# A graph attention layer on one core: the last product's output written by ScalarE, x added by accumulating transfers, the first norm tile by tile, and a fixed table as the order

## The chip, the cores and the metric

The kernel runs on one core of a Trainium2 chip. Its engines are TensorE (PE in the profile; its weight loads have a row of their own, PEld), VectorE (DVE), ScalarE (ACT), GpSimd (POOL) and SyncE (SP). Each works off its own list of instructions in order, and they meet only at semaphores. Transfers are issued from two lists: SP's (the hardware queue) and GpSimd's (the software queue, the one whose transfers can add to what stands at the destination). The metric is the time of one execution on the device in microseconds, the median of several.

## The reference

One pre-normalised layer of graph attention over 32 graphs of 512 nodes with 512 features, in float32:

```
h = jnp.maximum(_layernorm(x, axis=-1), 0.0)
x = x + _L0_gnn_ref(adj, h, W1, att_src1, att_dst1, b1, W2, att_src2, att_dst2, b2)

def gat_layer(x, mask, W, a_src, a_dst, bias, concat):
    xl = (x @ W).reshape(B, N, H, F)
    asrc = jnp.einsum('bnhf,hf->bnh', xl, a_src)
    adst = jnp.einsum('bnhf,hf->bnh', xl, a_dst)
    e = jax.nn.leaky_relu(asrc[:, :, None, :] + adst[:, None, :, :], NEG_SLOPE)
    e = jnp.where(mask[..., None], e, NEG_INF)
    attn = jax.nn.softmax(e, axis=1)
    out = jnp.einsum('bsdh,bshf->bdhf', attn, xl)
    return out (heads side by side, or their mean) + bias

mask = (adj > 0) | jnp.eye(N, dtype=bool)[None]
h = jax.nn.elu(gat_layer(x, mask, W1, att_src1, att_dst1, b1, concat=True))
h = gat_layer(h, mask, W2, att_src2, att_dst2, b2, concat=False)
```

The first layer has 4 heads of 256 features, the second one head of 512. What matters for the change is the last line of each graph: the second layer's product of attention and features, divided by the softmax's sums, plus x.

## The kernel before, in words

The work of a graph is cut into 128-row tiles (four of nodes, four of features). For each graph b the program does, in this order of dependence: `load` x and normalise it (`norm`: statistics on VectorE, 1/sqrt(var + eps) as a power on GpSimd, then scale, shift and relu on ScalarE; `norm_turn` turns the tiles for TensorE); `masks` (the adjacency as 0 or a large negative number, written to DRAM once); the first projection `project1`; the first layer's softmaxes (class `Soft`, one per head) and their products `gather1`; the second projection `project2`; the second layer's softmax `second_layer` and its product `gather2`, which ends with x added and the rows stored. A softmax tile p gets its mask by an accumulating transfer of 512 KB on GpSimd's list (`p<-dm`), and the sums by which it divides go through DRAM to be spread over the partitions (`drr<-rr`, then `rr<-drr`, on SP's list; `as<-das` likewise for the scores).

Most large products are done in seven block products instead of eight (`sevens`, a Strassen-Winograd scheme): products 1 to 7 are chains of matmuls into PSUM banks; some sums are kept in the bank, and a bank's sum goes on into another bank by a copy on ScalarE. Those copies are the rows `ACT ACTIVATE mm<-mm` of the profile. A bank is 2 KB per partition, and there are eight: a chain can start only when its bank has been read out.

`gather2` does so for the last product. Its inner function `put` (L1487) takes finished blocks of 128x256 from the bank to the output tile: on VectorE, bank times `share` (one over the softmax's sum) plus what stands in the tile. What stands there is x, which `residual` (L1435) has loaded ahead by SP into one of the four t tiles (or, for the last graphs, into tiles of adj, x and mt). After the row's last put SP stores it. The last graph goes through `gather2_plain` (L1514), which has no seven products.

The loop after L1560 interleaves the second half of one graph with the first of others. It doesn't run the work but adds jobs (engine, cost, what it reads and writes) to a `Program` (L223). `order` (L299) then sets the lists: a list scheduler with a clock of its own, in which each job has a modelled duration, each hand-over a modelled delay, and the two queues share a modelled wire. Where several jobs of an engine are ready, the smaller number in `PLACES` (L63) goes first; the places of one middle graph are repeated for all of them, each a turn later. So the lists of two middle graphs need not be alike. `emit` (L373) writes the instructions in that order, and the waits follow from what is read and written. All engines' instructions have one line each in the profile: L531 TensorE, L514 ScalarE, L517 VectorE, L520 SP's transfers, L525 GpSimd's transfers, L770 the power.

Of the kernel before, what the change touches and what calls it, by code (L numbers as in the profile page):

```python
# [10 lines left out]
F32 = mybir.dt.float32  # L11
# [4 lines left out]
OP = mybir.AluOpType  # L16
# [28 lines left out]
class Banks(Slots):  # L45
# [171 lines left out]
)  # L217
LATE = {
   
}  # L220

# [1488 lines left out]
```

## Time and profile before

| what | us |
|---|---|
| runs shown | 2767.8, 2768.55, 2772.54 |
| median | 2768.55 |
| profiled execution | 2769.33 |
| its span | 2767.6 |
| granted clock, mean | 0.999 |
| ScalarE puts of the last product | none |
| accumulating transfers on GpSimd's list | 314 masks of 512 KB |
| t<-in_x_dram on SP's list | 124 of 256 KB |

The profiled execution's own time is 1.73 us more than its span; what follows is counted from the span's start. In a group's row stand line, engine, operation, output<-input with the buffers' names, the shape, the count, and behind the bar the busy time, the mean in ns, and the idle time ahead with who ended it. In a timeline row stand the start, the duration, the engine and operation, and in brackets the idle time before and who ended it. A matmul's record is longer than the distance to the next one, since they are pipelined.

### The profile page before, as it was taken

To read this page: it belongs to the slowest core of one execution; us is meant where nothing else is said; L and a number is where in the kernel's file an instruction comes from. 1 tells how busy PE (TensorE), PEld (TensorE's weight loads), DVE (VectorE), ACT (ScalarE), POOL (GpSimd) and SP (SyncE) were. 2 spreads that over 40 slices of the span, in tenths; PEclk is the share of its full clock that TensorE was granted. 3 is DMA by queue.
4 is the path that set the end of the run, shared out by engine and by line. 5 is a ranking of instruction groups with operands and counts; after the bars stand their busy time and mean duration, and the time that the engine had idled before them with its cause. 6 is when DMAs were issued, how large, how long until landed. Compare 5 with 4: busy or idle time off the path is not lost. (4 is left out here: it accounts for less than half of the span.)

```text
span 2767.6 us, 42320 instructions
## 1 busy us (share of the span) xinstructions
PE 2742.4 (99%) x12924; PEld 2371.8 (86%) x12924; DVE 2558.2 (92%) x6732; ACT 2229.1 (81%) x4907; POOL 313.1 (11%) x356
## 2 busy tenths in 40 slices
PE   7999999999999999999999999999999999999999
PEld 6788888888888888888888888888888888888887
DVE  8999999999999999999999999999999999999996
ACT  5978888778887788877888877888778788788883
POOL 0110111101111111111011111111111111101110
PEclk9999999999999999999999999999999999999999
DMA  8657766667666667667676766766676767767563
GB/s 232 176 157 182 203 167 184 187 176 194 182 183 179 182 176 196 178 175 195 173 201 172 182 187 178 192 186 180 180 188 175 201 167 180 195 165 208 162 171 112
DMA packets 375864, 502.14 MB, mean 181 GB/s; under 512 B 222804, under 2 KB 227668, under 8 KB 375636
## 3 DMA queue, kind: packets, MB, share of 16 engines
q1 hardware_dynamic: 329844, 332.68, 42.4%
q0 software_dynamic: 45792, 166.74, 25.1%
q8 instruction: 103, 1.69, 0.3%
q14 instruction: 125, 1.02, 0.1%
HBM read 316.41 MB, written 51.31 MB: 133 GB/s over the span
## 5 line engine op out<-in xcount | busy, mean ns | idle before, releaser
L531 PE MATMUL mm<-w_sb,hs 128*128 128x257 f32 (+3 forms) x2908 | 667.0, 367 | 5.1 <-ACT mm L514 3.3
L531 PEld LDWEIGHTS mm<-w_sb,hs 128*128 128x128 f32 x2908 | 539.7, 190 | 87.7 <-ACT mm L514 6.7
L525 POOL DMA_DIRECT2D p<-dm x314 | 273.2, 875 | 2295.0 <-DVE p L517 764.3
L531 PE MATMUL mm<-w_sb,ht 128*128 128x258 f32 x2112 | 528.6, 382 | 2.7 <-ACT mm L514 2.5
L531 PE MATMUL mm<-p,xl 128*128 128x258 f32 (+1 forms) x1984 | 495.8, 383 | 0.1
L531 PE MATMUL mm<-w_sb,h 128*128 128x257 f32 x2056 | 477.8, 379 | 0.0
L517 DVE SCALAR_TENSOR_TENSOR p<-rr,z 128x512 f32<-128x512 f32 (+1 forms) x636 | 456.0, 742 | 2.4 <-DMA rr<-drr 2.4
L531 PEld LDWEIGHTS mm<-w_sb,ht 128*128 128x128 f32 x2112 | 393.7, 190 | 63.6 <-ACT mm L514 6.4
L514 ACT ACTIVATE p<-p,z 128x512 f32<-128x512 f32 (+1 forms) x636 | 433.4, 720 | 17.7 <-DVE p L517 12.4
L531 PEld LDWEIGHTS mm<-w_sb,h 128*128 128x128 f32 x2056 | 389.0, 189 | 58.4 <-ACT xl L514 0.5
L531 PEld LDWEIGHTS mm<-p,xl 128*128 128x128 f32 x1984 | 367.2, 190 | 52.7 <-issue 6.0
L514 ACT ACTIVATE mm<-mm 128x257 f32<-128x257 f32 (+2 forms) x498 | 169.8, 347 | 269.2 <-PE mm L531 236.2
L514 ACT ACTIVATE l<-as,z 128x512 f32<-128x512 f32 x516 | 354.4, 716 | 30.8 <-DMA as<-das 30.7
L514 ACT ACTIVATE l<-l,low 128x512 f32<-128x512 f32 x516 | 370.3, 721 | 7.6 <-DVE low L517 6.7
L517 DVE CUSTOM_DVE_ANT_1 l<-l,mt 128x512 f32<-128x512 f32 x516 | 346.2, 681 | 28.4 <-ACT l L514 27.4
L514 ACT ACTIVATE xl<-mm 128x258 f32<-128x258 f32 (+2 forms) x748 | 269.3, 382 | 91.4 <-PE mm L531 89.8
L514 ACT ACTIVATE h<-mm,b_sb 128x256 f32<-128x256 f32 (+1 forms) x504 | 231.0, 480 | 77.3 <-PE mm L531 76.6
L531 PE MATMUL mm<-t,hs 128*128 128x258 f32 (+1 forms) x992 | 246.1, 380 | 0.0
L517 DVE TENSOR_TENSOR xl<-xl,mm 128x258 f32<-128x258 f32 x372 | 155.3, 419 | 57.9 <-PE mm L531 48.3
L531 PEld LDWEIGHTS mm<-t,hs 128*128 128x128 f32 x992 | 185.8, 190 | 25.5 <-DVE t L517 0.2
L531 PE MATMUL mm<-xl,p 128*128 128x258 f32 (+2 forms) x752 | 189.7, 388 | 1.0 <-ACT h L514 0.6
L517 DVE SCALAR_TENSOR_TENSOR h<-xr,h 128x512 f32<-128x512 f32 x256 | 172.2, 683 | 6.1 <-ACT xr L514 6.1
(137 smaller groups left out, 3706.2 us busy)
## 6 DMA issues: line engine op xcount, KB each, us to landing
p<-dm POOLq DMA_DIRECT2D x314, 512.0 KB, 5.0
rr<-drr SPq DMA_DIRECT2D x159, 512.0 KB
x<-in_x_dram SPq DMA_DIRECT2D x129, 256.0 KB
adj<-in_adj_dram SPq DMA_DIRECT2D x128, 256.0 KB
as<-das SPq DMA_DIRECT2D x64, 512.0 KB
t<-in_x_dram SPq DMA_DIRECT2D x124, 256.0 KB
out_dram<-t SPq DMA_DIRECT2D x124, 256.0 KB
dm<-m SPq DMA_DIRECT2D x64, 256.0 KB
```

What stands on the lines that cost most here:

```text
L514: prog.add("ACT", cost, reads, writes, lambda: nc.scalar.activation(*a, **k))
L517: prog.add("DVE", cost, reads, writes, lambda: f(*a, **k))
L525: lambda: nc.gpsimd.dma_start(to, at, accum_op=OP.add), size,
L531: f(*a, **k)
```

## The change

**What `put` does.** Of the six products of `gather2` that reach the output tile, 3 and 7 stay on VectorE (bank times share, added to the tile), the others become a scaled copy on ScalarE that overwrites the tile. That moves 248 operations (31 graphs, 8 in each) from VectorE to ScalarE and leaves 124 on VectorE.

**Where x comes from.** `residual` loads x only for the last graph. For the others, after a row's last put, a transfer on GpSimd's list adds x from DRAM to the finished tile, and SP's store waits for it: 124 transfers of 256 KB leave SP's list, and 124 accumulating ones of the same size enter GpSimd's.

**The first norm.** For graph 0 the epsilon, the power and the shift run for each of the four tiles by itself (128x1 instead of 128x4), so each of these three instructions becomes four.

**Room.** The identity matrix for the turns takes the place of a work tile (`hx`) that is first used later; the constant `diag` is made from it there.

**The order.** The scheduler with its clock, the delays and the wire is gone, and so is the table `LATE`. `PLACES` has new numbers in a finer unit, and each engine's list is its jobs sorted by their place. All middle graphs then have the same list. The matmuls are the same in number and width.

```diff
-            dma(XLOAD, [x2_key(b, 0, 0)], halves, xr, x[b, d * P : (d + 1) * P, :])
+            if b == B - 1:
+                dma(XLOAD, [x2_key(b, 0, 0)], halves, xr, x[b, d * P : (d + 1) * P, :])
+            else:
+                for c in range(2):
+                    prog.alias(xk + (c,), [xk, xk + (c,)])
             XR[b].append((places[d], xk, xr))
...
             if n in (2, 5):
                 dve(TINY, [bk], [sk], nc.vector.reciprocal, share, ps[:, M : M + 1])
-            dve(
-                PUT, [bk, sk, xk + (c,)], [xk + (c,)], nc.vector.scalar_tensor_tensor,
-                to, ps[:, :M], share, to, op0=OP.mult, op1=OP.add,
-            )
+            if n in (3, 7):
+                dve(
+                    PUT, [bk, sk, xk + (c,)], [xk + (c,)], nc.vector.scalar_tensor_tensor,
+                    to, ps[:, :M], share, to, op0=OP.mult, op1=OP.add,
+                )
+            else:
+                act(COPY, [bk, sk, xk], [xk + (c,)], to, ps[:, :M], AF.Copy, scale=share)
 
             upper[u[0]] -= n in (2, 3)
             if n == 4 or r == 0 and upper[u[0]] == 0:
                 upper[u[0]] = -1
+                halves = [xk, xk + (0,), xk + (1,)]
+                accumulate(XADD, halves, halves, xt, x[b, d * P : (d + 1) * P, :])
                 dma(STORE, [xk, xk + (0,), xk + (1,)], (), out[b, d * P : (d + 1) * P, :], xt)
...
-        every = [sk + (t,) for t in range(NT)]
-        rstd = st[:, :, S + A]
-        dve(TINY, every, every, nc.vector.tensor_scalar_add, rstd, st[:, :, S + 1], EPS)
...
+        for ts in ([t] for t in range(NT)) if b == 0 else [range(NT)]:
+            every = [sk + (t,) for t in ts]
+            at = slice(ts[0], ts[-1] + 1)
+            rstd = st[:, at, S + A]
+            dve(TINY, every, every, nc.vector.tensor_scalar_add, rstd, st[:, at, S + 1], EPS)
+            prog.add(
+                "POOL", 1.0, every, every,
+                lambda r=rstd, n=len(every): nc.gpsimd.tensor_tensor(r, r, half[:, :n], op=OP.pow),
+            )
...
-    identf = sbuf.tile([P, P], F32, name="identf")
+    identf = hx[SMALL[0]][:, 0, :]
...
-                [xk], [pk], 0.44,
+                [xk, ("hx", SMALL[0])], [pk], 0.44,
...
     def order(self):
-        jobs, rank = self.jobs, self.ranks()
...
-                release(j, lambda s: t + jobs[j][1] + self.latency(j, s))
+        jobs, rank, done = self.jobs, list(self.ranks()), []
+        after, left = [[] for _ in jobs], [len(job[2]) for job in jobs]
...
+        lines = {e: [] for e in self.ENGINES}
+        for j in sorted(range(len(jobs)), key=lambda j: (rank[j], j)):
+            lines[jobs[j][0]].append(j)
+        lines = [deque(q) for q in lines.values()]
+        while any(lines):
+            q = min((q for q in lines if q and not left[q[0]]), key=lambda q: rank[q[0]])
+            j = q.popleft()
             done.append(j)
+            for k in after[j]:
+                left[k] -= 1
         return done
...
 PLACES = (
-    -21124, -21123, -21187, -21124, -19956, -19941, -19942, -21301, -19903, -19904, -18841, -19897, -6146, 6511,
...
 )
```

What moves in the lists is shown at three places. The first is VectorE's start before: four tiles of statistics, then one epsilon (`TENSOR_SCALAR`) and one shift for all, around the first score sums (`xr,w_sb<-w_sb,p`).

```order
L517 BN_STATS stats_123<-x_90 128x6
L517 BN_AGGR stats_123<-stats_123 128x2
L517 BN_STATS stats_123<-x_88 128x6
L517 BN_AGGR stats_123<-stats_123 128x2
L517 BN_STATS stats_123<-x_91 128x6
L517 BN_AGGR stats_123<-stats_123 128x2
L517 BN_STATS stats_123<-x_89 128x6
L517 BN_AGGR stats_123<-stats_123 128x2
L517 TENSOR_SCALAR stats_123<-stats_123 128x4
L517 SCALAR_TENSOR_TENSOR xr_96,w_sb<-w_sb,p_102 128x256
```

The same start with the change:

```order
L473 BN_STATS stats_122<-x_90 128x6
L473 BN_AGGR stats_122<-stats_122 128x2
L473 TENSOR_SCALAR stats_122<-stats_122 128x1
L473 BN_STATS stats_122<-x_88 128x6
L473 BN_AGGR stats_122<-stats_122 128x2
L473 TENSOR_SCALAR stats_122<-stats_122 128x1
L473 BN_STATS stats_122<-x_87 128x6
L473 BN_AGGR stats_122<-stats_122 128x2
L473 TENSOR_SCALAR stats_122<-stats_122 128x1
L473 BN_STATS stats_122<-x_89 128x6
L424 TENSOR_SCALAR diag<-hx_79 128x128
L473 SCALAR_TENSOR_TENSOR stats_122<-stats_122 128x1
```

The epsilon of each tile now follows its own statistics, and the first tile's shift (the last row) stands ahead of the fourth tile's aggregation. The second place is GpSimd's list in a middle graph, where before there were only masks and one power for each graph (`L770`).

```order
L525 DMA p_102<-dm_120 128x1024 x2
L525 DMA p_103<-dm_122 128x1024 x2
L525 DMA p_104<-dm_122 128x1024 x2
L770 TENSOR_TENSOR stats_123<-stats_123,half 128x4
L525 DMA p_102<-dm_122 128x1024 x2
L525 DMA p_103<-dm_122 128x1024 x2
```

And with the change (t_105 to t_108 are the output tiles):

```order
L481 DMA p_103<-dm_120 128x1024 x2
L481 DMA t_105<-in_x_dram 128x512
L481 DMA t_107<-in_x_dram 128x512
L481 DMA p_101<-dm_120 128x1024
L481 DMA t_108<-in_x_dram 128x512
L481 DMA t_106<-in_x_dram 128x512
L729 TENSOR_TENSOR stats_123<-stats_123,half 128x4
L481 DMA p_101<-dm_120 128x1024
L481 DMA p_102<-dm_120 128x1024 x2
```

The four accumulating transfers of a graph stand together, and one mask's two halves (p_101) are parted by two of them. The third place is SP's list around the stores of a middle graph, before:

```order
L520 DMA rr_114<-drr_118 128x1024
L520 DMA out_dram<-t_108 128x512
L520 DMA x_90<-in_x_dram 128x512
L520 DMA out_dram<-t_106 128x512
L520 DMA out_dram<-t_109 128x512
L520 DMA out_dram<-t_107 128x512
L811 DMA_TRANSPOSE x_91<-adj_94 128x8x128
L520 DMA drr_119<-rr_115 4x8x32
L811 DMA_TRANSPOSE x_90<-adj_95 128x8x128
L520 DMA rr_115<-drr_119 128x1024
```

And with the change:

```order
L476 DMA rr_114<-drr_118 128x1024
L476 DMA x_87<-in_x_dram 128x512
L476 DMA out_dram<-t_108 128x512
L476 DMA drr_117<-rr_113 4x8x32
L476 DMA out_dram<-t_105 128x512
L476 DMA out_dram<-t_107 128x512
L476 DMA out_dram<-t_106 128x512
L770 DMA_TRANSPOSE x_87<-adj_94 128x8x128
L770 DMA_TRANSPOSE x_88<-adj_93 128x8x128
L476 DMA rr_113<-drr_117 128x1024
```

The broadcast of a softmax's sums (`rr_113<-drr_117`) now stands behind three stores and two transposes, and each store behind its tile's accumulating transfer; before, the write and the read of the broadcast both stood behind the stores, and the stores waited only for VectorE.

More of the change, by code (lines that the diff above doesn't have):

```diff
@@ L2 @@
 from contextlib import ExitStack
-from heapq import heappop, heappush
 import concourse.bass as bass
@@ L63 @@
 PLACES = (
[153 rows of a table removed]
-)
-LATE = {
-}
[197 rows of a table added]
+)
 class Program:
-    CROSS, SAME = 0.15, 0.07
-    PAIRS = {("PE", "ACT"): 0.21, ("PE", "DVE"): 0.21, ("DVE", "POOL"): 0.58, ("POOL", "DVE"): 0.4}
-    AHEAD, MASK, OTHER = 3.5, (0.75, 1.84), 0.76
-    KIND = {
-        0.3: (0.39, 1.21, 0.1, 0.9),
-        0.76: (0.81, 1.62, 0.33, 0.64),
-        0.77: (0.44, 1.45, 0.2, 0.82),
-        0.9: (0, 1.72, 1.0, 0.41),
-        0.92: (0.48, 2.18, 0.24, 0.89),
-        0.94: (-0.2, 1.76, 0.21, 0.6),
-        1.09: (1.58, 1.56, 0.53, 0.59),
-        1.84: (0.48, 2.18, 0.24, 0.89),
-        2.23: (0.58, 1.62, 0.53, 0.4),
-    }
     ENGINES = "PE", "ACT", "DVE", "POOL", "SP"
@@ L267, in alias @@
         self.readers[key] += [self.writer[k] for k in others if k in self.writer]
-    def latency(self, a, b):
-        if self.jobs[a][0] != self.jobs[b][0]:
-            return self.PAIRS.get((self.jobs[a][0], self.jobs[b][0]), self.CROSS)
-        return 0.0 if self.jobs[a][0] == "PE" else self.SAME
-    def kind(self, j):
-        if self.jobs[j][0] == "POOL":
-            return self.MASK
-        return self.KIND.get(self.jobs[j][4], self.KIND[self.OTHER])
     def ranks(self):
@@ L286, in ranks @@
         turn = sum(job[1] for job in self.jobs[first : first + each] if job[0] == "PE")
-        rank, self.place = [], []
         for j in range(n):
             if j < first:
-                v, i = j, 0
+                yield PLACES[j] / 10000
             elif j < last:
-                v, i = first + (j - first) % each, (j - first) // each + 1
+                yield PLACES[first + (j - first) % each] / 10000 + turn * ((j - first) // each + 1)
             else:
-                v, i = first + each + j - last, (last - first) // each + 1
-            self.place.append(v)
-            rank.append(PLACES[v] / 100 + turn * i)
-        return rank
+                yield PLACES[first + each + j - last] / 10000 + turn * ((last - first) // each + 1)
     def order(self):
-        jobs, rank = self.jobs, self.ranks()
-        n = len(jobs)
-        after = [[] for _ in range(n)]
+        jobs, rank, done = self.jobs, list(self.ranks()), []
+        after, left = [[] for _ in jobs], [len(job[2]) for job in jobs]
         for j, job in enumerate(jobs):
@@ L305, in order @@
                 after[d].append(j)
-        left = [len(job[2]) for job in jobs]
-        ready_at, self.start, done = [0.0] * n, [0.0] * n, []
-        free, soon, ready = dict.fromkeys(self.ENGINES, 0.0), defaultdict(list), defaultdict(list)
-        wires, now, behind = {"SP": deque(), "POOL": deque()}, 0.0, {"SP": 0.0, "POOL": 0.0}
-        for j in range(n):
-            if not left[j]:
-                heappush(soon[jobs[j][0]], (0.0, j))
-        def release(j, at):
-            for s in after[j]:
-                ready_at[s] = max(ready_at[s], at(s))
-                left[s] -= 1
-                if not left[s]:
-                    heappush(soon[jobs[s][0]], (ready_at[s], s))
@@ L321, in step @@
-        def step(until):
-            nonlocal now
-            busy = [q for q in wires if wires[q] and wires[q][0][1] <= now]
-            speed = dict.fromkeys(wires, 1.0)
-            if len(busy) == 2:
-                speed["SP"], speed["POOL"] = self.kind(wires["SP"][0][0])[2:]
-            event, which = until, None
-            for q in wires:
-                if wires[q]:
-                    j, since, todo = wires[q][0]
-                    t = now + todo / speed[q] if q in busy else since
-                    if t < event:
-                        event, which = t, q
-            for q in busy:
-                wires[q][0][2] -= (event - now) * speed[q]
-                behind[q] -= (event - now) * speed[q]
-            now = event
-            if which in busy:
-                j = wires[which].popleft()[0]
-                release(j, lambda s: event + self.kind(j)[1] + LATE.get(self.place[j], 0) / 100)
-            return which is not None
@@ L344, in order @@
-        while len(done) < n:
-            t, e = float("inf"), None
-            for q in self.ENGINES:
-                if ready[q]:
-                    at = free[q]
-                elif soon[q]:
-                    at = max(free[q], soon[q][0][0])
-                else:
-                    continue
-                if q in wires:
-                    at = max(at, now + behind[q] - self.AHEAD)
-                if max(at, now) < t:
-                    t, e = max(at, now), q
-            if step(t):
-                continue
-            while soon[e] and soon[e][0][0] <= t:
-                k = heappop(soon[e])[1]
-                heappush(ready[e], (rank[k], k))
-            j = heappop(ready[e])[1]
-            self.start[j] = t
-            free[e] = t + jobs[j][1]
-            done.append(j)
-            if jobs[j][4] is not None:
-                wires[e].append([j, free[e] + self.kind(j)[0], jobs[j][4]])
-                behind[e] += jobs[j][4]
-            else:
-                release(j, lambda s: t + jobs[j][1] + self.latency(j, s))
+        lines = {e: [] for e in self.ENGINES}
@@ L443, in tile_gat @@
     nc.scalar.preload_act_table_set("natural_log_exp_and_others")
-    identf = sbuf.tile([P, P], F32, name="identf")
-    make_identity(nc, identf)
-    diag = sbuf.tile([P, P], BF16, name="diag")
-    nc.vector.tensor_scalar(diag, identf, -1.0, BIG, op0=OP.add, op1=OP.mult)
     half = sbuf.tile([P, NT], F32, name="half")
@@ L468, in tile_gat @@
     hx = {n: sbuf.tile([P, 3, P], F32, name=f"hx{n}") for n in SMALL}
+    identf = hx[SMALL[0]][:, 0, :]
+    make_identity(nc, identf)
+    diag = sbuf.tile([P, P], BF16, name="diag")
+    nc.vector.tensor_scalar(diag, identf, -1.0, BIG, op0=OP.add, op1=OP.mult)
     rs = sbuf.tile([P, 2, 2, 2], F32, name="rs")
@@ L764, in norm @@
             dve(TINY, [sk + (t,)], [sk + (t,)], nc.vector.bn_aggr, st[:, t, S : S + A], st[:, t, :S])
[L765 to L776 removed]
+        for ts in ([t] for t in range(NT)) if b == 0 else [range(NT)]:
[7 more added lines that the diff above has]
+            )
+            shift = st[:, at, S]
+            dve(
+                TINY, every, every, nc.vector.scalar_tensor_tensor,
+                shift, shift, -1.0, rstd, op0=OP.mult, op1=OP.mult,
+            )
         ST[b] = sk, st
```

12 lines of the change are left out of this document (3 added, 9 removed), and 349 rows, old and new, of the table PLACES.

## The prediction

> **What bounds the kernel now.** I read the page's busy table first, then the same table cut into five stretches, then who waits for whom in the long middle stretch, and last the timelines where TensorE stands.
>
> ```profile
> span 2767.6 us, 42320 instructions
> PE 2742.4 (99%) x12924; PEld 2371.8 (86%) x12924; DVE 2558.2 (92%) x6732; ACT 2229.1 (81%) x4907; POOL 313.1 (11%) x356
> 0.00:50.00 50.00, 36.09 (x171) 31.07 (x172) 39.96 (x164) 23.57 (x48) 2.86 (x8) 1.00 0.94 271
> 50.00:250.00 200.00, 198.47 (x879) 161.38 (x878) 184.58 (x515) 169.33 (x370) 26.41 (x28) 0.99 0.65 170
> 250.00:2620.00 2370.00, 2365.14 (x11250) 2062.82 (x11248) 2216.07 (x5766) 1950.71 (x4294) 271.66 (x306) 1.00 0.69 183
> 2620.00:2700.00 80.00, 78.79 (x367) 67.32 (x367) 74.17 (x180) 64.09 (x150) 10.39 (x12) 1.00 0.63 170
> 2700.00:2768.00 68.00, 63.88 (x264) 49.26 (x262) 43.40 (x110) 21.38 (x49) 1.75 (x2) 0.99 0.33 106
> ```
>
> After the bounds of a stretch come its length, the busy time of TensorE (matmuls, weight loads), VectorE, ScalarE and GpSimd, the clock, and the share of the DMA engines. TensorE is busy 99% of the span at full clock, so no work taken from VectorE shortens anything by itself; only TensorE's idle time can be won or lost. It is 25.2 us: 13.9 in the first 50, 1.53 up to 250, 4.86 in the whole middle, 1.21 up to 2700 and 4.1 behind it. The change leaves every matmul in place (12,960 passes in both instruction lists; the trace lacks a few records), so these are the whole field for a gain. A loss has no such limit.
>
> The waits of the middle stretch (engine and line, whom it waited for; us in total, times, longest):
>
> ```profile
> PEld mm L531 <- ACT mm L514: 10.7, 17, 1.6
> PE mm L531 <- ACT mm L514: 4.4, 8, 1.2
> DVE t L517 <- PE mm L531: 5.9, 20, 0.3
> ACT mm L514 <- DVE t L517: 26.4, 28, 1.8
> POOL p L525 <- DVE p L517: 591.0, 92, 15.5
> ACT p L514 <- DMA p<-dm: 5.2, 8, 1.4
> ```
>
> What TensorE waits for there is ScalarE's copies of one matmul bank into another, and nothing else of weight. Here is how one such wait comes about, and how another is fed by a late mask:
>
> ```profile
> 852.53 1.95 ACT L514 ACTIVATE l<-as,z 128x512 f32<-128x512 f32 x3 [2.27 <-DMA as<-das]
> 854.38 0.52 ACT L514 ACTIVATE mm<-mm 128x129 f32<-128x129 f32 x2
> 854.69 2.01 PE L531 MATMUL mm<-w_sb,ht 128*128 128x258 f32 x8 [0.81 <-ACT mm L514]
> 2351.29 8.79 DMA p<-dm
> 2360.10 1.16 ACT p L514 x2
> 2361.34 0.27 ACT mm L514
> 2361.65 0.49 PE L531 MATMUL mm<-w_sb,hs 128*128 128x129 f32 x2 [0.45 <-ACT mm L514]
> 2385.74 233.85 PE mm L531 x1104
> ```
>
> At 852.53 three long operations stand ahead of the copy, because their input landed late, and TensorE stands 0.81 us. At 2360 the same with two exponentials behind a late mask. So the order on ScalarE's list sets the small stalls. A wait also costs more than the idle shows: a matmul record lasts some 0.38 us and the next starts after 233.85/1104 = 0.212, so up to 0.17 us of each of these 25 waits is hidden under the matmul before it. The middle thus holds 4.86 + 25 x 0.17 = about 9 us at most.
>
> **The start.**
>
> ```profile
> 8.15 0.66 DVE L517 BATCH_NORM_STATS2 stats<-x 128x6 f32<-128x512 f32 x1
> 9.31 1.04 POOL L770 TENSOR_TENSOR stats<-stats,half 128x4 f32<-128x4 f32 x1 [8.00 <-DVE stats L517]
> 11.20 2.23 ACT L514 ACTIVATE x<-x,stats 128x512 f32<-128x512 f32 x3 [9.16 <-DVE stats L517]
> 13.21 0.43 DVE L517 SCALAR_TENSOR_TENSOR xr<-w_sb,p 128x256 f32<-128x256 f32 x1 [1.30 <-DMA p<-in_L_gnn_att_dst_dram]
> 12.06 2.82 PE L531 MATMUL mm<-identf,x 128*128 128x128 f32 x12 [12.06 <-ACT x L514]
> 14.67 5.92 PE L531 MATMUL mm<-w_sb,ht 128*128 128x258 f32 x24
> 20.43 0.60 PE L531 MATMUL mm<-identf,x 128*128 128x128 f32 x4
> ```
>
> Before, one power on GpSimd (9.31) waits for all four tiles' statistics, the first normalisation starts at 11.20 and TensorE at 12.06. Tile by tile, three of the four powers can run before the last tile's statistics end at about 9.0. Even if each 128x1 power takes the 1.04 us of the 128x4 one, the four end by about 10.4 and the first normalisation starts soon after the second tile. But the transposes were not the last gate: the score sum that waits for att_dst starts at 13.21 and takes 0.43, and the first product needs it. That landing is a load in the same place of SP's list. So the products can start near 13.7 in place of 14.67, 1.0 us; and with four transposes done by then the group at 20.43 no longer stands in the dense run, 0.44 to 0.60. I take 1.5 us. Bounds: 0, if VectorE's later sums set the pace as the waits of this stretch allow, and 14.67 - 12.06 = 2.6, if nothing but the transposes did.
>
> **The puts moved to ScalarE, and x's way into the tile.**
>
> ```profile
> L517 DVE SCALAR_TENSOR_TENSOR t<-mm,rs,t 128x256 f32<-128x256 f32 x360 | 165.6, 474 | 8.9 <-PE mm L531 7.6
> L514 ACT ACTIVATE mm<-mm 128x256 f32<-128x256 f32 x124 | 46.5, 375 | 70.3 <-PE mm L531 68.5
> L514 ACT ACTIVATE h<-mm,b_sb 128x256 f32<-128x256 f32 x496 | 225.7, 477 | 77.0 <-PE mm L531 76.6
> L525 POOL DMA_DIRECT2D p<-dm x314: 862/862/1217, 63.0 to 2718.9; - x157
> p<-dm POOLq DMA_DIRECT2D x314, 512.0 KB, 5.0
> q1 hardware_dynamic: 329844, 332.68, 42.4%
> q0 software_dynamic: 45792, 166.74, 25.1%
> ```
>
> VectorE loses 248 operations of 0.474, 117.6 us, and goes from 92% to 88% busy. ScalarE gains 248. A scaled copy to SBUF is not in this trace; its bounds are the bank copy of the same size (375 ns) and the activation with a bias that reads a bank and writes SBUF (477). That is 93 to 118 us, and 81% becomes 84 to 85%. The second is the nearer row, as it writes to SBUF too. On TensorE's path neither counts: a bank is released 0 to 0.1 us later or earlier, and the 26.4 us that ScalarE stood behind VectorE's puts (28 times, once a graph) goes, because the put ahead of that copy is now its own.
>
> GpSimd gains 124 accumulating transfers of 256 KB. Issuing one costs 862 ns (the middle value of the masks' 314), 107 us, so 11% becomes 15%. On the wire a mask takes 25.1% x 2767.6 / 314 = 2.2 us of all 16 engines (what little else shares that queue is counted with it); x's transfer moves half the bytes of a mask's row, so 1.1 to 2.2. SP loses 124 loads: its queue moved 332.68 MB in 42.4% of 2767.6 us, so 0.26 MB takes 0.9 us. The net is +0.2 to +1.3 us times 124, 1 to 6 points of a 69% share. An accumulate lands in about 4 to 5 us by the mask's 5.0, and the store that follows it waits that long on SP's list. Nothing of TensorE's reads the tile; what could be hurt is what stands behind it: the next masks on GpSimd, and the broadcasts on SP. In the new order the four accumulates stand in one group, with one mask pair parted by them, where there was none; by the order's lists 100 passes or more of TensorE lie between a row's last product and the reuse of its tile, 100 x 0.212 = 21 us, against 5 + 2 for accumulate and store. The masks of the second layer have some 73 passes, 15 us, between their last use and their next. Value for the middle from this: 0, between -1 and +2, the latter if five covers run out by one 0.4 us wait each.
>
> The page "SBUF — State Buffer" of the Trainium skill, section "SBUF: two separate sides", speaks against this move: a transfer issued from GpSimd starves for descriptors while VectorE holds the shared port, and SP's or ScalarE's queue is advised. By its case of 3.1 us in place of 0.62 an issue would be an estimated 2.5 us later, four accumulates 10 us, and the masks behind them would have 5 of 15 us left. The trace disagrees so far: with VectorE at 92% the issues stay at 862 ns and the longest at 1217. I sum by the trace.
>
> **The order.** The list scheduler with modelled times goes, and each engine's list is a fixed table. In the lists, places where a ScalarE piece must finish while only one product chain (four passes, 0.85 us) runs are 173, down from 380, VectorE's 157 against 155. That is the kind of place of the 25 waits above. If waits fall with places, 9 x (1 - 173/380) = 4.9 us go; some new ones come, since the new list can't give way to whatever lands first in a model. I take -4, with 0 to -9 as bounds. For the run-in (50 to 250, idle 1.53, and the rest of the first 50, about 1.9 behind the start) I take -1.2, between +1.5 and -3.4; for 2620 to 2700 -0.5 of its 1.21.
>
> **The end.** The final product and store stay:
>
> ```profile
> 2749.97 13.91 PE L531 MATMUL mm<-xl,p 128*128 128x512 f32 x32
> 2763.92 0.69 DVE L517 TENSOR_TENSOR t<-mm,t 128x512 f32<-128x512 f32 x1 [1.89 <-PE mm L531]
> 2756.64 8.33 SPq L520 DMA_DIRECT2D out_dram<-t  x4
> ```
>
> The last graph still loads x and adds it on VectorE, so its tail is the same 3.7 us. Its x tiles must wait for the stores of the graph before, which now wait for their accumulates: +0.2, up to +0.5.
>
> **Sum.** -1.5 (start) - 1.2 - 4 - 0.5 + 0.2 = -7.0 on the profiled execution's 2769.33: 2762.3. The median of the runs shown, 2768.55, is 0.78 lower, so 2761.6.
>
> **Rivals.**
>
> *Only the start is won.* The table merely trades one set of small stalls for another: -1.5, 2767.0. For it: 4.86 of 2370 us is little, and each fixed place that comes late is late in every graph. Against it: the places with one chain of cover halve.
>
> *Masks and broadcasts behind x (slower).* GpSimd's queue is in order; an accumulate that waits for its row's last put holds the masks behind it, and a store that waits for an accumulate holds the softmax's broadcast on SP. A late mask cost 0.45 us at 2361 with 8.79 us of wire in the chain above. One to two such places in each of 29 middle graphs are +13 to +26, +20 in the middle, less the start's 1.5: about 2787. For it: masks went out 92 times in wait of VectorE, up to 15.5 us each, so the queue is used late. Against it: 21 us of cover, and ScalarE waited for a mask only 8 times, 5.2 us in all. It decides once a mask's cover falls below its 5 us landing.
>
> *GpSimd's issues stretch (slower).* With five issues in a row, each at the longest 1217 in place of 862 ns, a mask goes out 1.8 us later. If that uses up one cover in each graph, 31 x 0.45 = +14, less the start's 1.5: about 2781. Against it: the 314 issues of this trace reach 1217 at the longest, beside a VectorE that will be less busy. This is where the skill's page would lead, if its rule held here.
>
> *ScalarE's copies come later (slower).* At 85% a copy that frees a bank stands behind one more put of 0.48 us. Cover is 0.85 us in 173 places; if one place in each graph loses 0.3 us, +9: about 2776. Against it: the puts are placed apart from the copies, and 26.4 us of ScalarE's standing behind VectorE end.
>
> *The change does not do what it says*, in that x's transfers take the wire from SP's loads. At +6 points of 69% no stretch but the first (94%, without such transfers) is near full; 2769 at most, and I count it with the first rival.
>
> **How the numbers follow.** A difference under 0.2% (5.5 us: 2763.0 to 2774.1) can't be told from no change. Forecast 0.60, with its own range 2755 to 2767; about three quarters of it lies below 2763.0, so 0.45 faster, 0.15 same. Only the start 0.19, same but for 0.01 faster. Masks and broadcasts 0.11, stretched issues 0.03, both slower. ScalarE's copies 0.07: slower 0.06, same 0.01. Together faster 0.46, same 0.34, slower 0.20. The range 2754 to 2778 holds the forecast's own range, the second case and that of the copies, and leaves out most of the masks' and the stretched issues' cases, 0.12, and about 0.04 of the forecast's gains.
>
> **What would show it.** Right: first normalisation before 10 us and products by 13.8; ScalarE at 84 to 85%, VectorE at 88%; TensorE's idle in 250 to 2620 below 3 us with fewer than 15 waits for ScalarE's copies; no wait of TensorE behind a mask. Wrong: a wait on the weight loads that returns each graph; exponentials that wait for masks more than 20 times; broadcasts landing late behind stores; or accumulate issues well over 862 ns.

## The result and the profile after

The changed kernel takes 2839.21 us (median of 4 runs, 2836.63 to 2840.43) against 2770.55 for the kernel before: ratio 1.0247, 95% interval 1.0229 to 1.0264. The forecast was 2761.6, with 2778 as the upper end. The profiled execution took 2836.63, its span is 2834.9, 67.3 us more than before. Three executions in all stand far above the others of their kernel (3603.89 us in e7, 7325.82 in e5 and one of 4141.77 of the kernel before) and are left out of the ratios and medians below.

The page's busy table of the changed kernel, and its first three stretches (length, then busy time of matmuls, weight loads, VectorE, ScalarE, GpSimd, then clock and DMA share):

```profile
span 2834.9 us, 42850 instructions
PE 2767.0 (98%) x12924; PEld 2367.5 (84%) x12924; DVE 2464.9 (87%) x6490; ACT 2334.1 (82%) x5155; POOL 451.2 (16%) x483
0.00:50.00 50.00, 38.22 (x181) 32.52 (x181) 40.98 (x172) 23.90 (x49) 4.15 (x11) 1.00 0.90 264
50.00:250.00 200.00, 197.22 (x866) 158.36 (x867) 182.96 (x505) 170.62 (x375) 29.03 (x32) 1.00 0.66 171
250.00:2620.00 2370.00, 2327.14 (x10968) 2007.80 (x10968) 2073.77 (x5396) 1991.64 (x4395) 388.12 (x407) 1.00 0.71 178
```

TensorE's idle time in the middle is 42.9 us where it was 4.86, and 282 fewer matmuls fit into the same 2370 us. ScalarE gained 105 us of work, as forecast (93 to 118), and is busy 82% of the longer span (81% before); VectorE lost 93, not 117.6, and went from 92% to 87%. The clock is 1.00 as before. So the loss is waiting, in every graph. One row that both kernels have gives the length of a graph, VectorE's first sum of a first-layer operand (29 of them, one a graph; the first and last start are behind the durations), before and after:

```profile
L517 DVE TENSOR_TENSOR hs<-p x29: 691/693/693, 179.5 to 2563.9; 128x512 f32<-128x512 f32 x29
```

```profile
L473 DVE TENSOR_TENSOR hs<-p x29: 691/693/694, 175.8 to 2626.7; 128x512 f32<-128x512 f32 x29
```

(2563.9 - 179.5) / 28 = 85.16 us a graph before, (2626.7 - 175.8) / 28 = 87.53 after. 28 x 2.37 = 66 of the 67 us are there. The same quotient serves for the experiments. Who waited for whom in the middle stretch of the changed kernel:

```profile
DVE t L473 <- DMA out_dram<-t: 94.0, 20, 6.7
PEld mm L487 <- ACT f L470: 33.0, 27, 1.2
PE mm L487 <- ACT f L470: 27.9, 27, 1.0
PEld mm L487 <- DVE xl L473: 20.8, 31, 1.8
PE mm L487 <- DVE xl L473: 9.0, 21, 1.4
PEld mm L487 <- ACT h L470: 10.0, 27, 0.4
```

None of these was among the first rows of before. The weight loads (PEld) tell the loss more fully than the matmuls: all their waits in this stretch come to 82 us, against 15 before, and the difference has the size of the loss. (A matmul's record is longer than the distance to the next one, so it covers part of a wait.) There are two large places. The first is a copy f of half a bank by ScalarE, for which TensorE stands 1.0 us once in every graph. The timelines of TensorE and ScalarE around one of them:

```profile
1031.26 0.39 PE L487 MATMUL mm<-wx,hx 128*128 128x129 f32 x2
1032.68 0.49 PE L487 MATMUL mm<-w_sb,hs 128*128 128x129 f32 x2 [1.03 <-ACT f L470]
1031.74 0.71 ACT L470 ACTIVATE p<-p,z 128x512 f32<-128x512 f32 x1
1032.36 0.27 ACT L470 ACTIVATE f<-mm 128x129 f32<-128x129 f32 x1
```

f reads one half of the bank, the matmul that waits writes the other half. Before, the same two products stand next to each other too, and the second does not wait. TensorE's list with its waits, before, then after:

```order
L531 MATMUL mm_133<-wx_85,hx_86 128x129 [waits Activation_49]
L531 MATMUL mm_133<-w_sb,hs 128x129
L531 MATMUL mm_135<-t_106,hs 128x258 [waits DVE_49]
L531 MATMUL mm_135<-t_106,hs 128x256
L531 MATMUL mm_132<-w_sb,hs 128x129 [waits Activation_49]
```

```order
L487 MATMUL mm_131<-w_sb,ht 128x258
L487 MATMUL mm_132<-wx_78,hx_79 128x129 [waits Activation_49]
L487 MATMUL mm_132<-w_sb,hs 128x129 [waits Activation_49]
L487 MATMUL mm_135<-p_102,xl 128x256 x2
L487 MATMUL mm_134<-t_105,hs 128x258 [waits DVE_49]
```

The second wait is new. Waits follow from the order in which instructions of different engines are written out. Before, that was the modelled order of time, and the product came ahead of f. Now the sorted lists are merged by their numbers, f has the smaller one and is written out ahead of the product, and the product waits for f; the experiment e7 below reverses just this.

The second place is the output tile. The path of one graph's tiles, from four timelines: VectorE's last put, two groups of x's transfers, the stores, VectorE's next use of a tile, and TensorE behind it:

```profile
1068.21 0.48 DVE L473 SCALAR_TENSOR_TENSOR t<-mm,rs,t 128x256 f32<-128x256 f32 x1
1068.52 2.14 POOL L481 DMA_DIRECT2D t<-in_x_dram  x2
1073.07 0.86 POOL L481 DMA_DIRECT2D p<-dm  x1 [2.42 <-DVE p L473]
1073.61 2.11 POOL L481 DMA_DIRECT2D t<-in_x_dram  x2
1081.04 0.34 SPq L476 DMA_DIRECT2D out_dram<-t  x1
1084.89 0.69 DVE L473 TENSOR_TENSOR t<-p 128x512 f32<-128x512 f32 x1 [4.90 <-DMA out_dram<-t]
1091.19 2.00 PE L487 MATMUL mm<-t,hs 128*128 128x258 f32 x8 [0.42 <-DVE xl L473]
t<-in_x_dram POOLq DMA_DIRECT2D x120, 256.0 KB, 7.1
```

The tile that SP stores first and VectorE uses first, t_108, gets x third, behind a mask that itself waits 2.42 us. Its transfer goes out at 1073.6, and such transfers land 7.1 us after their issue (the last row, a median; 4 to 5 was assumed by the masks' 5.0). The store is issued at 1081.04 and VectorE released at 1084.89, 3.9 us later, where 2 was assumed. From issue to release that makes 11.3 us in place of 7, and VectorE stands 4.9 us in front of its sum into the tile. The Trainium skill's page "DMA: Bandwidth & Descriptors", section "Anatomy of one DMA — SWDGE (gpsimd) path", would give 2.0 us and the bytes by 436 GB/s, an estimate of 2.6 us; these transfers, which add and stand two by two behind masks in one queue, took 7.1.

The start came out near the forecast. GpSimd and TensorE there:

```profile
8.45 0.55 POOL L729 TENSOR_TENSOR stats<-stats,half 128x1 f32<-128x1 f32 x1 [0.46 <-DVE stats L473]
10.07 1.97 PE L487 MATMUL mm<-hx,x 128*128 128x128 f32 x8 [10.07 <-ACT x L470]
13.95 8.35 PE L487 MATMUL mm<-w_sb,ht 128*128 128x258 f32 x37
```

### The profile page after: what moved, and what is told of

Its sections match the earlier page's. It is cut to its first block, busy times and chain, and to the rows that moved or that the text cites. A ratio compares the mean times of both kernels' runs of the same rounds, so it can differ in the third digit from the quotient of the medians.

```text
span 2834.9 us, 42850 instructions
## 1 busy us (share of the span) xinstructions
PE 2767.0 (98%) x12924; PEld 2367.5 (84%) x12924; DVE 2464.9 (87%) x6490; ACT 2334.1 (82%) x5155; POOL 451.2 (16%) x483
## 5 line engine op out<-in xcount | busy, mean ns | idle before, releaser
L481 POOL DMA_DIRECT2D p<-dm x314 | 280.8, 897 | 2269.3 <-DVE p L473 1097.8
L487 PE MATMUL mm<-p,xl 128*128 128x258 f32 (+1 forms) x1984 | 512.3, 384 | 7.7 <-issue 5.9
L470 ACT ACTIVATE p<-p,z 128x512 f32<-128x512 f32 (+1 forms) x636 | 441.3, 717 | 37.5 <-DMA p<-dm 17.3
L487 PE MATMUL mm<-t,hs 128*128 128x258 f32 (+1 forms) x992 | 253.2, 382 | 7.8 <-DVE xl L473 7.0
L473 DVE TENSOR_TENSOR t<-p 128x512 f32<-128x512 f32 x122 | 83.6, 685 | 130.1 <-DMA out_dram<-t 98.4
```

Of the source, the lines that this page charges most:

```text
L470: prog.add("ACT", cost, reads, writes, lambda: nc.scalar.activation(*a, **k))
L473: prog.add("DVE", cost, reads, writes, lambda: f(*a, **k))
L481: lambda: nc.gpsimd.dma_start(to, at, accum_op=OP.add), size,
L487: f(*a, **k)
```

## The experiments

Every ratio is to runs of the kernel before on the same chip; they lie between 2766.4 and 2768.7 us in the median. What a run wins or loses against the changed kernel is told by the difference of the ratios (1.0247 for the changed kernel), times 2768 us, since the chips differ by some us; each ratio's interval is some 4 to 7 us to either side. The expectations go by the medians and so have 23 for e1 and 76 for e6, where the ratios give 21 and 78.

**Leave x's transfers out, or give the puts back** (e1, e2).

```diff
-                accumulate(XADD, halves, halves, xt, x[b, d * P : (d + 1) * P, :])
+                prog.add("POOL", 0.95, halves, halves, lambda: None, XADD)
```

> The changed kernel without the 124 accumulating transfers: the output of graphs 0 to 30 lacks x; the stores then wait only for the puts, and every list is otherwise the same. Theory T (tiles come free late): in the changed kernel VectorE stands 4.9 us in each middle graph until a store of an output tile has landed, because x's transfer lies between the last put and the store; without it that wait is under 1 us a graph, TensorE's excess of about 2.4 us a graph goes, and the time is 2765 to 2780. Theory S (ScalarE is overloaded by 248 more operations): ScalarE's list is unchanged, so 2825 to 2840. Theory L (the fixed lists are bad by themselves, whatever the transfers do): 2815 to 2840.

Measured: 2816.21, ratio 1.0171 (1.0151 to 1.0191); 86.87 us a graph. VectorE's wait is gone and 21 us with it, but two thirds of the loss stay. Theory T names one part only; f's wait stands unchanged in that trace (27 times 1.0 us).

```diff
-                act(COPY, [bk, sk, xk], [xk + (c,)], to, ps[:, :M], AF.Copy, scale=share)
+                prog.add("ACT", COPY, [bk, sk, xk], [xk + (c,)],
+                         lambda: nc.vector.tensor_scalar_mul(to, ps[:, :M], share))
```

> The changed kernel with the 248 moved puts given back to VectorE as a multiplication into the tile; x still comes by accumulating transfers, the lists keep their places. Theory S: ScalarE is back at about 78% busy and the copies come earlier, so 2775 to 2800. Theory T: VectorE still waits for the stores and has 118 us more to do, so 2835 to 2870, with the wait for the stores still above 3 us a graph. Theory L: 2830 to 2860.

Measured: 2943.02, ratio 1.0629 (1.0608 to 1.065), slower than any of the three theories had it. Giving the puts back costs 106 us more: VectorE's list was laid out without these 248 operations, and TensorE now waits for VectorE's hs in every graph (63.4 us in all, 26 times). So the run does not show what ScalarE's load costs.

**The transfers earlier, for two tiles** (e6: t_108 ahead of the second layer's masks, t_106 ahead of t_105, and one store moved).

```diff
+PLACES[1542] = PLACES[1450] - 500; PLACES[1550] = PLACES[1546] - 50; PLACES[1551] = PLACES[1543] + 1
```

> The changed kernel with another place for two of the four accumulating transfers of a middle graph, and for one store: the tiles that VectorE needs first (t_108, then t_106) get their x first, t_108 ahead of the second layer's two mask transfers. Nothing else changes. Theory T: the wait of VectorE for the stores falls from 4.9 us to under 1.5 us a graph and the time by 29 x 1.5 to 2.4 us, to 2765 to 2795. Theories S and L: 2820 to 2840, with the copies as late as before.

Measured: 2914.92, ratio 1.0528 (1.0512 to 1.0543), the wrong way. Its waits say why:

```profile
POOL t L481 <- ACT l L470: 552.3, 24, 23.3
ACT p L470 <- DMA p<-dm: 89.4, 72, 3.5
PEld mm L487 <- DVE xl L473: 76.6, 27, 4.6
```

GpSimd stands 23 us a graph at a transfer whose put on ScalarE (behind an l there) isn't done, the masks behind it go out late, ScalarE waits 72 times for a mask (17 in the changed kernel), and TensorE up to 4.6 us for a sum of VectorE's that stands behind those exponentials. This is the recorded rival of the masks behind x, brought about by three numbers.

**The old scheduler with the new table** (e3).

```diff
-class Program: sorted lists, PLACES[v] / 10000
+class Program: the scheduler of the kernel before, PLACES[v] / 10000 as priorities, LATE = {}
```

> The changed kernel's program and its table, but the lists made by the scheduler of before, with its modelled durations and wires and the table's places as priorities (the corrections that it had for single places are left out). Theory L: the fixed lists are the loss, so 2765 to 2785. Theory T: the scheduler gives way to whatever is ready in its model, so VectorE's sums are put behind other work when the tile is late; but the model doesn't know a landing of 7 us, so part remains: 2785 to 2820. Theory S: 2815 to 2840.

Measured: 2837.57, ratio 1.0245 (1.0228 to 1.0262), as slow as the changed kernel, but through other waits (VectorE waits for the stores only 3 times between 500 and 2500 us). It doesn't tell the theories apart: the new table is no set of priorities for that scheduler.

**The wait for f alone** (e7), every engine's list unchanged row for row:

```diff
+                prog.hold.append((halves[n, us], len(prog.jobs)))     # f, the product behind it
...
+        for f, q1 in self.hold:
+            after[q1].append(f)
+            left[f] += 1
```

> The changed kernel with the same instructions in the same order on every engine; only the order in which two instructions of different engines are written out is turned round: ScalarE's copy f of one half of a bank now comes behind TensorE's next product into the other half, as in the kernel before, so that ScalarE waits for that product and not that product for the copy. Theory W (a wait that the new way of merging the lists adds): in the changed kernel and in e1_no_xadd TensorE stands 1.0 us before that product in each middle graph (and 0.17 us hidden); without the wait 30 x 0.9 to 1.2 us go: 2803 to 2815, and no wait of TensorE for f. Theory S (ScalarE late altogether): the stall moves to the next products, whose banks ScalarE also frees: 2828 to 2840.

Measured: 2799.12 (2797.17 to 2807.02), ratio 1.0119 (1.0095 to 1.0142): 35 us less than the changed kernel, the upper end of theory W's gain. No wait of TensorE for f is left.

**One transfer moved within its group** (e9: t_108's goes first, behind the same masks).

```diff
+PLACES[1542] = PLACES[1546] - 80
```

> The changed kernel with one of the four accumulating transfers of a middle graph moved: that of t_108, the tile VectorE writes first, goes first in the group and no longer third, behind the same masks as before. Theory T: t_108's store can go some 4 us earlier, VectorE's wait of 4.9 us a graph falls below 1 us, and the time by 10 to 23 us (leaving the transfers out altogether, e1_no_xadd, won 23): 2816 to 2830. If the masks behind the group are what counts (e6_pool_order, with two transfers ahead of masks, cost 76 us): 2835 to 2850.

Measured: 2818.38, ratio 1.0181 (1.0166 to 1.0196): 18 us, nearly all that leaving the transfers out had won. VectorE's wait is halved, though not under the 1 us that theory T asked for, and that was enough: the weight loads behind VectorE's xl wait 1.9 us in all, where it was 20.8.

```profile
DVE t L473 <- DMA out_dram<-t: 43.3, 24, 2.5
```

**The two together**, without x (e10) and with it (e11).

> e1_no_xadd and e7_f_after together: no accumulating transfers of x (the output of graphs 0 to 30 lacks x) and the copy f written out behind the product. If the two causes add up (T and W): 2816 less 27 to 36, 2780 to 2790. If the order has further stalls of that size that these two hid: 2795 to 2816.

Measured: 2780.03, ratio 1.0047 (1.0027 to 1.0066).

> e7_f_after and e9_x_swap together; the whole computation is done. T and W adding up: 2784 to 2804. If they hide one another's gain: 2804 to 2825.

Measured: 2785.33, ratio 1.0059 (1.0041 to 1.0077). 35 + 18 = 53 us were to be had, 52 came: the causes add up. The graph is down to 85.59 us. What TensorE's weight loads still wait for in the middle is led by ScalarE:

```profile
PEld mm L490 <- ACT h L473: 10.0, 27, 0.4
PEld mm L490 <- ACT t L473: 5.9, 27, 0.4
PEld mm L490 <- ACT ht L473: 2.9, 12, 0.3
PEld mm L490 <- ACT mm L473: 1.7, 3, 0.7
```

The copies into another bank (mm), 10.7 us before, have nearly gone; h and t come once in each graph. The t are the puts that the change gave to ScalarE.

**The end** (e12: the last graph's first store behind two loads of x).

```diff
+PLACES[2370] = PLACES[2358] + 1
```

> e11_f_and_swap with one transfer of SP moved at the end: the first store of the last graph goes behind the loads of x for its last two tiles and no longer ahead of them. In e11_f_and_swap those loads are issued at 2771.5, behind that store's wait, and TensorE's last matmul ends at 2777.2, the span at 2783.7, 6.6 us later against 3.7 in the kernel before. If that store is the cause, the 2.9 us go: 2782; else no change from 2785.

Measured: 2785.16, ratio 1.0057 (1.0041 to 1.0072), no change. In this trace the loads still wait for the stores of an earlier graph's rows, and VectorE's last three sums for them (3.94 us). The longer end has not been traced to one row.

**The parts alone, the old scheduler making new lists** (e4: last product; e5: first norm).

> The kernel before, with its scheduler and its table, and only the last product changed: puts 1, 2, 4, 5 and 6 on ScalarE, x added by accumulating transfers (their place is that of the row's store), no load of x. If the move itself costs nothing and the loss lies in the table and in how the lists are merged: 2760 to 2780. If the accumulating transfers cost by themselves, as tiles that come free late (they cost 23 us in the changed kernel): 2785 to 2800. If ScalarE's 248 operations were the loss: above 2800.

> The kernel before with the first norm tile by tile and nothing else; its scheduler makes new lists from that, so small stalls elsewhere move too. The recorded prediction says 1.5 us faster (0 to 2.6), the first product near 13.7 us; the changed kernel has it at 13.95. If only att_dst's landing counts, within 1 us of before; if the new lists decide, anything from -5 to +10.

Measured: 3203.36, ratio 1.1559 (1.1528 to 1.159), and 3118.60, ratio 1.1255 (1.1229 to 1.1281), far outside every case. In e5 nine tiny instructions in the first 10 us cost 347 us, because the scheduler gives way differently from there on: graphs are 87 to 114 us long, and the granted clock is 0.967 (0.963 in e4). So both tell nothing of the parts.

**The parts alone in the old lists held fast** (e13: last product; e14: first norm; e15: both). The order is made from the old jobs; only what a job writes out differs:

```diff
-            dve(PUT, [bk, sk, xk + (c,)], [xk + (c,)], nc.vector.scalar_tensor_tensor, ...)
+            prog.add("DVE", PUT, [bk, sk, xk + (c,)], [xk + (c,)],
+                     lambda: nc.scalar.activation(to, ps[:, :M], AF.Copy, scale=share))
...
-                dma(STORE, [xk, xk + (0,), xk + (1,)], (), out[b, d * P : (d + 1) * P, :], xt)
+                    nc.gpsimd.dma_start(xt, at, accum_op=OP.add)
+                    nc.sync.dma_start(o, xt)
```

> The kernel before with its own lists held fast and only the first norm done tile by tile (TensorE, ScalarE and SP row for row as before). The recorded prediction's term: -1.5 us, between 0 and -2.6, first product near 13.7 us in place of 14.67. If later sums on VectorE set the pace: 0. e5_before_norm, the same edit with the lists made anew, cost 354 us; if that came from the edit and not from the lists, this one is above 2800 too.

Measured: 2767.31, ratio 1.0000 (0.9990 to 1.0009). The first product starts at 13.83 us, but the gain is too small to be told from none.

> The kernel before with its own lists held fast: TensorE's list is the same row for row, and the others too but for the last product's edit, each instruction at the place of the one it replaces (248 puts on ScalarE where VectorE's stood, no loads of x into the output tiles, an accumulating transfer just ahead of each store). If the edit costs nothing by itself and the loss lies in the new order: 2762 to 2778. If the transfers make the tiles late wherever they stand (23 us in the changed kernel): 2780 to 2800. If ScalarE's longer list delays its copies: above 2800, with TensorE's waits for ScalarE's copies several times the 25 of before.

Measured: 3083.83, ratio 1.1145 (1.1128 to 1.1163), the third case (above 2800) by its size, and TensorE's waits for ScalarE's copies into another bank are 70 where there were 25. But these come to 34 us only; the long waits are for xl, once in a graph. The waits, and one graph's chain from four timelines:

```profile
SPq L1515 <- DMA t<-in_x_dram: 435.0, 66, 11.8
DVE stats L517 <- DMA x<-in_x_dram: 209.6, 25, 9.7
PE mm L531 <- ACT xl L514: 178.0, 25, 8.5
1064.64 0.34 SPq L1515 DMA_DIRECT2D out_dram<-t  x1
1065.07 1.14 SPq L520 DMA_DIRECT2D x<-in_x_dram  x1
1073.89 0.69 DVE L517 BATCH_NORM_STATS2 stats<-x 128x6 f32<-128x512 f32 x1 [9.65 <-DMA x<-in_x_dram]
1075.22 0.72 ACT L514 ACTIVATE l<-l,low 128x512 f32<-128x512 f32 x1 [8.77 <-DVE low L517]
1078.91 3.79 PE L531 MATMUL mm<-w_sb,h 128*128 128x257 f32 x8 [8.50 <-ACT xl L514]
```

SP stands at the first store until x has been added; the load of an x tile for a later norm stands right behind; VectorE stands 9.65 us at its statistics, ScalarE 8.8 behind VectorE, TensorE 8.5 behind ScalarE. In the lists of before that store waited for VectorE alone. Not all of the 315 us is waiting: the granted clock, 0.999 before, is 0.967 over this span. In the graph shown it is 1.00 up to 1072, then 0.61, 0.50 and 0.61 in three stretches of 4 us, then 1.00 again; from 1080 to 1084 TensorE does 13 matmuls, in the next 4 us 20. Nearly every graph has such a stretch. The graphs are 95.31 us long, 10.15 more than before, of which the wait makes 8.5; the rest, an estimate of 1.7 us a graph, is about what the lower clock takes.

> e13_lists_xadd and e14_lists_norm together: all that the changed kernel computes differently, in the lists of before. The sum of the two; what is then left to the changed kernel's 2839 is the new order and the wait it adds.

Measured: 3079.95, ratio 1.1129 (1.1097 to 1.1161): the same as e13 within its noise, as the sum of the two should be.

**Two rows of SP exchanged** (e16: e13 with the x load ahead of the first store, once a graph). The last of these exchanges falls between two transfers of the same tile, so 128 rows of graph 29 are stored with the tile's next contents.

```diff
-out_dram<-t_108, x_90<-in_x_dram, out_dram<-t_106
+x_90<-in_x_dram, out_dram<-t_108, out_dram<-t_106
```

> e13_lists_xadd (3084) with two neighbouring transfers of SP's list exchanged once in each graph: the load of an x tile for the next norm goes ahead of the graph's first store, as in the changed kernel's table, and no longer behind it; every other list is row for row that of e13. Theory Q (SP's list is held by the store that waits for x's accumulating transfer): in e13 VectorE's statistics wait 9.7 us for that load in each graph and TensorE 8.5 us at the end of that chain, so 29 x 7 to 8.7 us go: 2830 to 2880. If the transfers themselves or ScalarE's puts are the loss of e13: above 3000.

Measured: 2908.26, ratio 1.0505 (1.0488 to 1.0523): 176 us back for two rows, somewhat less than theory Q's 200 to 250. The chain above is gone, and the clock is back at 0.996, which is part of the gain. The wait of the changed kernel comes forth, and TensorE's weight loads wait for ScalarE's copies 68 times, where it was 17 times and 10.7 us before:

```profile
DVE t L529 <- DMA out_dram<-t: 140.1, 26, 6.4
DVE stats L529 <- DMA x<-in_x_dram: 3.1, 6, 0.6
PEld mm L543 <- ACT mm L526: 63.7, 68, 1.5
```

## Why the prediction was wrong, step by step

**The order** (forecast -4, bounds 0 to -9). This step failed most. It counted places where a ScalarE piece must finish within one product chain, and found fewer. That count follows what the program's own table of reads and writes names. The wait for f is not in it, for there the two halves of the bank are apart; it arises when the instructions are written out. It stood in TensorE's list with its waits, and cost 35 us (e7). The part that was counted came out as forecast: the weight loads' waits for copies into another bank fell from 10.7 to 1.5 us in the middle. A wait on the weight loads that returns each graph was one of the recorded signs of being wrong, and it is what came. The upper bound, 0, was set by the sight of old waits; a new list can bring new ones in every graph.

**The cover of the output tile** (forecast 0, -1 to +2). The step set 21 us of TensorE's passes against 5 + 2 us for transfer and store. Three things failed. VectorE's sum into the tile stands well ahead of TensorE's use (1079.99 without the wait, against 1091.19 in the graph shown), and VectorE's list is in order, so cover ends there. The transfer doesn't start at the last put, but behind masks that wait for VectorE. And transfer and store take 7.4 + 3.9 us there, not 5 + 2. The term put at 0 is 18 to 21 us (e9, e1).

**ScalarE and VectorE off the path.** Right in the sizes: a put takes 466 ns, between the 375 and 477 assumed, and ScalarE's extra work of 105 us lies within 93 to 118. e11 takes back 52 of the 68 us and leaves every put on ScalarE, so ScalarE's load is not the main loss. It is not nothing either: f, h, ht and t, for which TensorE's weight loads wait, are all ScalarE's. The forecast looked for copies into another bank alone, and its rival of late copies (0.07, +9) has about the size of what stays in e11, though it is not shown that the puts make them late.

**GpSimd's issues.** Assumed 862 ns; x's took 1219 in the median, 1634 at the longest. The Trainium skill's page "SBUF — State Buffer", section "SBUF: two separate sides", had warned of transfers issued from GpSimd. The masks' issues stay at 865 ns in the median beside the same VectorE, so a starving of all that GpSimd issues is not seen, and no run here settles what makes x's longer.

**Masks and broadcasts behind x** (chance 0.11, 2787). The mechanism is real, and of more weight than was given: three table numbers make it cost 78 us (e6), and in the lists of before a store on SP's list, which holds a load of x and not a broadcast, makes the edit cost 315 (e13). The new table had put that load ahead of the store; in e16 this alone gave 176 of them back. For the changed kernel itself it was not the cause: ScalarE waited for masks 17 times, against 8.

**The start** (-1.5). Near the forecast in its place: first product at 13.95, in place of 14.67, where 13.7 was forecast. That att_dst's landing gates it is not shown: its sum is done by 12.80, and in both kernels the first product follows the transposes without an idle time of TensorE. What the start is worth can't be told from nothing (e14: ratio 1.0000, 0.9990 to 1.0009, so at most some 3 us).

**The end** (+0.2). Too small. TensorE's last matmul ends 6.1 us ahead of the span's end, where it was 3.7: VectorE's last three sums wait 4.45 us for their x. That these loads are late because the rows of the graph before now need one transfer more is likely but not shown; e12 moved one store and did not shorten the end.

**What stays open.** e11 is 16 us slower than before. Its graphs are 85.59 us long, 0.43 more than before, which makes 12 us; without x's transfers (e10) they are 85.55, so that rest lies in the table or ScalarE's puts, not in the transfers. TensorE's weight loads wait 25 us in the middle of e11, 10 more than before, and 18.8 of them for ScalarE's h, t and ht. That points to ScalarE, but whether its pieces are late by the places in the table or by the 248 puts among them was not tried apart. Of the other 4 us some 3 are at the end.

## What to carry to other kernels

Where a hand-made order is merged from several lists, read the waits that come out, row by row, next to those of the old order: two neighbouring instructions of different engines, written out the other way round, cost 35 us here with every list unchanged. Count the cover of a buffer to the next instruction that stands for it on any in-order list, not to the engine that matters in the end. And before a store is made to wait for one more transfer, look at what stands behind it in its queue.

## What the runs showed that was not expected

Lists that are made anew can cost far more than the edit that caused it: nine instructions of 0.15 to 1 us ahead of everything, and a scheduler that reacts to them, cost 347 us (e5), while the same nine in unchanged lists cost nothing that can be measured (e14).

A long wait of TensorE cost more than its length: in a wait of 8.5 us that ended at 1078.9 the granted clock fell to 0.50, and it was back at 1.00 only at 1084 (e13). The changed kernel's waits, 1.8 us at the longest in its middle, left it at 1.00.

An accumulating transfer of 256 KB, two of them behind a mask, took 7.1 us in the median from issue to landing, while the mask of 512 KB took 5.0.
